# A second matrix product as seven products of combined quarters, in a two-layer graph network kernel

## The chip, the cores and the metric

The kernel runs on one core of one Trainium2 chip. The metric is device microseconds of one execution. The kernel before took 2775.54 us, the median of three runs from 2774.79 to 2775.55. The profile is of one further execution, whose span from the first to the last instruction is 2774.7 us.

## The reference

Two layers are applied to `x`, 16 batches of 1024 nodes with 256 channels, all in fp32. Layer 0 is an attention whose queries come from a weighted adjacency product; it isn't touched. Layer 1 is a graph convolution with two dense products and two batch norms:

```python
agg = jnp.einsum('nm,bmd->bnd', A_hat, features)
x = agg.reshape(-1, d)
h = jax.nn.relu(_batchnorm(x @ W1.T + b1, g1, be1))
out = h @ W2.T + b2
out = _batchnorm(out, g2, be2)
```

`W1` is 512 x 256 and `W2` 256 x 512. The layer's input is added to `out`. The change concerns `h @ W2.T + b2`, which per batch is a product of a 256 x 512 matrix with a 512 x 1024 one, in the transposed form that the kernel uses (channels on the partitions).

## The kernel before, in words

The function `layers` makes layer 0 and the first part of layer 1: adjacency product, `W1` product and bias. It leaves the result in device memory as 32 arrays `y1_d[i]` of 128 x 4 x 512 (two halves of 512 nodes for each of 16 batches, four chunks of 128 hidden channels), and the layer's input as `x1_d[b]`. The statistics for the first batch norm are gathered on the way, on VectorE. The last writes of `y1_d` are issued from the GpSimd queue (line 497).

The function `second` does the rest, and is where the change lies. Its order is the order of the code, as written by hand; each engine works through its own queue in that order and waits on semaphores.

- `affine` (lines 831 to 840) turns mean and variance into scale and shift. Its reciprocal square root runs on GpSimd (lines 80 and 81), three small operations follow on VectorE.
- For each of 32 half batches `i`, `load_y` (line 864, SP queue) brings 1 MB into one of three buffers of pool `io`; `relu` (line 870, ScalarE) applies the batch norm and the ReLU in place, chunk by chunk; `product` (line 878, TensorE) makes two products of 128 output channels x 512 nodes, each a sum over four chunks of `W2`, in one of four PSUM banks. One fp32 matmul of the code appears as two records in the trace. `keep` (lines 889 and 890, VectorE) adds the bias, which moves the result from PSUM to a resident tile `y2`, and takes its statistics.
- On the way five tiles `x1_d[b]` are loaded ahead by `load_x1` (line 850). Those beyond the five use the `io` buffers once these are free.
- Then the second batch norm: `bn_aggr` (line 921), `affine`, and for each batch a scale and shift on ScalarE (line 928), transposes on TensorE (line 940), the sum with `x1` on VectorE (line 946), and one write of 1 MB from the GpSimd queue (line 947). The next `x1` tile is loaded when a write has freed its buffer.

`look` and `flag`, called once in the middle of the loop, test whether layer 0's exponentials stayed in range; a second pass after that test isn't taken in the runs shown.

Of the kernel before, what the change touches and what calls it, by code (L numbers as in the profile page):

```python
# [10 lines left out]
F32 = mybir.dt.float32  # L11
AF = mybir.ActivationFunctionType
ALU = mybir.AluOpType
# [4 lines left out]
P = 128  # L18
# [5 lines left out]
def gnn_two_layers_kernel(  # L24
# [12 lines left out]
    nc = tc.nc  # L37
    B, N, C = x.shape
    H1 = w1_t.shape[1]
    NT = N // P  # L40
    CC = C // P
    HC = H1 // P
    HD = C // HEADS
    FB = 512
    NH = N // FB
# [15 lines left out]
    w2 = const.tile([P, HC, C], F32, name="w2")  # L61
    b1, g1, be1 = (vec[:, i * HC : (i + 1) * HC] for i in range(3))
    b2, g2, be2 = (vec[:, 3 * HC + i * CC : 3 * HC + (i + 1) * CC] for i in range(3))
    stats1 = const.tile([P, HC, B * NH, 6], F32, name="stats1")
    mv1 = const.tile([P, HC, 2], F32, name="mv1")
    stats2 = const.tile([P, CC, B * NH, 6], F32, name="stats2")
# [11 lines left out]
    def rsqrt(dst, src, add, tmp):  # L78

        nc.gpsimd.tensor_scalar_add(tmp, src, add)  # L80
        nc.gpsimd.tensor_tensor(dst, tmp, neg_half[:, : dst.shape[1]], op=ALU.pow)
# [740 lines left out]
    def second(kind):  # L822

        st = ExitStack()
        wp = st.enter_context(tc.tile_pool(name=f"wp_{kind}", bufs=1))
        yp = st.enter_context(tc.tile_pool(name=f"yp_{kind}", bufs=1))
        xp = st.enter_context(tc.tile_pool(name=f"xp_{kind}", bufs=5))
        io = st.enter_context(tc.tile_pool(name=f"io_{kind}", bufs=3))
        ps = st.enter_context(tc.tile_pool(name=f"ps_{kind}", bufs=4, space=PSUM))

        def affine(mv, gamma, beta, name):

            n = mv.shape[1]
            sm = wp.tile([P, 4, n], F32, name=f"sm_{name}")
            s, sh, rstd, tmp = (sm[:, i, :] for i in range(4))
            rsqrt(rstd, mv[:, :, 1], EPS, tmp)
            nc.vector.tensor_mul(s, rstd, gamma)
            nc.vector.tensor_mul(sh, mv[:, :, 0], s)
            nc.vector.tensor_sub(sh, beta, sh)
            return s, sh  # L840

        xos = []

        def load_x1():


            b = len(xos)
            pool, tag = (xp, "xo") if b % 8 < 5 else (io, "yin")
            xo = pool.tile([P, NT, C], F32, tag=tag, name=f"xo_{kind}_{b}")
            nc.sync.dma_start(out=xo, in_=x1_d[b])  # L850
            xos.append(xo)

        with st:
            y2 = [yp.tile([P, CC, N], F32, name=f"y2_{kind}_{b}") for b in range(B)]
            JH = HC // 2
            aff = []
            for half in range(2):
                r = slice(half * JH, (half + 1) * JH)
                aff.append(affine(mv1[:, r], g1[:, r], be1[:, r], f"1{half}"))
            ys, pzs = {}, {}  # L860

            def load_y(i):
                ys[i] = io.tile([P, HC, FB], F32, tag="yin", name=f"yin_{kind}_{i}")
                nc.sync.dma_start(out=ys[i], in_=y1_d[i])

            def relu(i, half):
                s1, sh1 = aff[half]
                for j in range(JH):
                    y = ys[i][:, half * JH + j, :]
                    nc.scalar.activation(  # L870
                        y, y, AF.Relu, bias=sh1[:, j : j + 1], scale=s1[:, j : j + 1]
                    )

            def product(i, k, half):
                if half == 0:
                    pzs[i, k] = ps.tile([P, FB], F32, tag="pz", name=f"pz_{kind}_{i}_{k}")
                for j in range(half * JH, (half + 1) * JH):
                    nc.tensor.matmul(  # L878
                        pzs[i, k],
                        w2[:, j, k * P : (k + 1) * P],  # L880
                        ys[i][:, j, :],
                        start=(j == 0),
                        stop=(j == HC - 1),
                    )

            def keep(i, k):
                b, g = divmod(i, NH)
                dst = y2[b][:, k, g * FB : (g + 1) * FB]
                nc.vector.tensor_scalar_add(dst, pzs[i, k], b2[:, k : k + 1])
                nc.vector.bn_stats(stats2[:, k, i, :], dst)  # L890

            for i in range(3):
                load_y(i)

            for half in range(2):
                for i in range(2):
                    relu(i, half)
                for i in range(2):
                    for k in range(CC):
                        product(i, k, half)  # L900
                        if half == 1:
                            keep(i, k)
            for i in range(2, B * NH):
                if i > 2:
                    load_y(i)
                if i % 4 == 3 and len(xos) < 5:
                    load_x1()
                for half in range(2):
                    relu(i, half)
                for k in range(CC):  # L910
                    for half in range(2):
                        product(i, k, half)
                    keep(i, k)
                if kind == "f" and i == B * NH // 2:
                    look()
                if kind == "f" and i == B * NH // 2 + 3:
                    flag(ps.tile([P, FB], F32, tag="pz", name=f"good_{kind}")[:, 0:1])

            mv2 = wp.tile([P, CC, 2], F32, name="mv2")
            for k in range(CC):  # L920
                nc.vector.bn_aggr(mv2[:, k, :], stats2[:, k].rearrange("p a s -> p (a s)"))
            s2, sh2 = affine(mv2, g2, be2, "2")
            for b in range(B):
                while len(xos) < min(b + 8, B):
                    load_x1()
                xo = xos[b]
                for k in range(CC):
                    nc.scalar.activation(
                        y2[b][:, k, :],
                        y2[b][:, k, :],  # L930
                        AF.Identity,
                        bias=sh2[:, k : k + 1],
                        scale=s2[:, k : k + 1],
                    )
                for g in range(NT // 2):
                    pt = ps.tile([P, 2, C], F32, tag="pz", name=f"pt_{kind}_{b}_{g}")
                    for j in range(2):
                        t = 2 * g + j
                        for k in range(CC):
                            nc.tensor.transpose(  # L940
                                pt[:, j, k * P : (k + 1) * P],
                                y2[b][:, k, t * P : (t + 1) * P],
                                ident,
                            )
                    dst = xo[:, 2 * g : 2 * g + 2, :]
                    nc.vector.tensor_add(dst, pt, dst)
                nc.gpsimd.dma_start(out=out[b].rearrange("(t p) c -> p t c", p=P), in_=xo)  # L947
# [6 lines left out]
    def look():  # L954

        nc.vector.tensor_reduce(ext[:, 0:1], seen[:, 0, :], AX.X, ALU.max)
        nc.vector.tensor_reduce(ext[:, 1:2], seen[:, 1, :], AX.X, ALU.min)
        nc.vector.tensor_scalar(ext[:, 0:1], ext[:, 0:1], 1e25, None, op0=ALU.is_le)
        nc.vector.tensor_scalar(ext[:, 1:2], ext[:, 1:2], 1e-30, None, op0=ALU.is_ge)
        nc.vector.tensor_mul(ext[:, 2:3], ext[:, 0:1], ext[:, 1:2])  # L960

    def flag(good):

        nc.tensor.matmul(good[0:1, :], ext[:, 2:3], ones[:, 0:1], start=True, stop=True)
        nc.vector.tensor_scalar(bad, good[0:1, :], -1.0, float(P), op0=ALU.mult, op1=ALU.add)

    with tc.manual_schedule():
        layers(False)
        second("f")

    again = nc.values_load(bad[0:1, 0:1], min_val=0, max_val=P)  # L971
    with tc.If(again > 0):
        layers(True)
        second("s")
# [37 lines left out]
```

## Time and profile before

| | time, us |
|---|---|
| median of three runs | 2775.54 |
| span of the profiled execution | 2774.7 |
| TensorE busy | 2700.8 (97%) |
| VectorE busy | 1610.3 (58%) |
| ScalarE busy | 1277.1 (46%) |
| GpSimd busy | 190.8 (7%) |
| first matmul of line 878 starts, last one ends | 2467.04, 2689.05 |
| first transpose of line 940 starts | 2695.43 |
| first and last write of line 947 are issued | 2701.05, 2758.33 |

In the profile PE is TensorE's matmul, PEld its weight load, DVE VectorE, ACT ScalarE, POOL GpSimd and SP the queue that issues most loads. A group of instructions is given as line, engine, operation, output <- inputs with partitions x elements and type, a count, and then busy microseconds, mean nanoseconds of one, and the idle time of that engine just before the group, with what ended it. In the timeline each row is a start, a length, engine, line and operation, and in brackets the idle time before it with what ended it. A window gives for each engine the busy microseconds and instructions, then the clock that TensorE was granted, the busy share of the DMA engines and the GB/s moved.

### The profile page before, as it was taken

The page shows a single profiled execution, that of the slowest core. Times are in us where ns is not written, and L with a number is a line of the kernel's source. Part 1 is how long each engine was busy: PE and PEld are TensorE (multiplying, and loading weights), DVE is VectorE, ACT ScalarE, POOL GpSimd, SP SyncE. Part 2 cuts the span into 40 slices and gives each one's busy share as a digit, 9 for nine tenths or more (in the row PEclk, how much of TensorE's full clock was granted, in tenths as well). Part 3 has the DMA queues.
Part 4 walks back from the last instruction along what each step waited for, and adds up shares of the span by engine and source line. Part 5 has one row for each costly group of instructions (what it writes and reads, how often), then busy time and mean ns, then how long its engine had stood idle before and what let it go on. Part 6 is the DMA issues. An engine that isn't in the chain of part 4 may idle for free. (4 is left out here: it accounts for less than half of the span.)

```text
span 2774.7 us, 31770 instructions
## 1 busy us (share of the span) xinstructions
PE 2700.8 (97%) x12426; PEld 999.5 (36%) x12426; DVE 1610.3 (58%) x2426; ACT 1277.1 (46%) x1811; POOL 190.8 (7%) x320
## 2 busy tenths in 40 slices
PE   7999999999999999999999999999999999999984
PEld 3333333333333333333333333333333333334443
DVE  5665655656565656566565656565565656634444
ACT  5654544535353635444453536354443534334443
POOL 0100100000000001000000000010100001100001
PEclk9999999999999999999999999999999999999997
DMA  4612223122232223231322322232313212245449
GB/s 152 208 50 84 99 80 107 73 97 86 92 107 76 95 81 106 84 103 65 105 77 92 106 84 91 85 105 76 107 61 114 77 61 77 96 162 198 167 148 351
DMA packets 106976, 297.35 MB, mean 107 GB/s; under 512 B 9536, under 2 KB 26432, under 8 KB 98624
## 3 DMA queue, kind: packets, MB, share of 16 engines
q1 hardware_dynamic: 88640, 223.91, 23.8%
q0 software_dynamic: 18176, 71.31, 6.8%
q8 instruction: 100, 1.64, 0.2%
q14 instruction: 60, 0.49, 0.1%
HBM read 223.88 MB, written 71.30 MB: 106 GB/s over the span
## 5 line engine op out<-in xcount | busy, mean ns | idle before, releaser
L641 ACT ACTIVATE p<-sc 128x1024 f32<-128x1024 f32 x512 | 496.3, 1021 | 719.4 <-PE sc L633 719.4
L663 DVE TENSOR_TENSOR acc<-acc,p 128x1024 f32<-128x1024 f32 x384 | 469.5, 1223 | 193.0 <-ACT p L641 172.7
L633 PE MATMUL sc<-q,k 64*128 64x512 f32 x2048 | 510.6, 617 | 0.5 <-ACT p L641 0.5
L674 PE MATMUL o<-p,v 128*64 128x512 f32 x2048 | 497.5, 607 | 0.0
L146 PE MATMUL pa<-aht,h_b 128*64 128x512 f32 x2048 | 455.9, 592 | 0.0
L146 PE MATMUL pg<-w,h_a 128*64 128x512 f32 x2048 | 453.5, 592 | 1.1 <-DVE q L401 1.1
L633 PEld LDWEIGHTS sc<-q,k 64*128 64x128 f32 x2048 | 176.6, 186 | 321.8 <-issue 280.8
L146 PEld LDWEIGHTS pg<-w,h_a 128*64 128x64 f32 x2048 | 148.0, 137 | 293.3 <-issue 282.7
L146 PEld LDWEIGHTS pa<-aht,h_b 128*64 128x64 f32 x2048 | 146.9, 137 | 286.6 <-issue 284.3
L700 DVE RECIPROCAL inv<-sums 128x128 f32<-128x128 f32 x256 | 221.7, 917 | 24.5 <-PE sums L691 24.5
L146 PE MATMUL py<-at,w 128*64 128x512 f32 x1024 | 230.6, 592 | 0.8 <-ACT y L496 0.8
L674 PEld LDWEIGHTS o<-p,v 128*64 128x64 f32 x2048 | 124.4, 136 | 286.6 <-issue 286.4
L878 PE MATMUL pz_f<-yin_f,w 128*128 128x512 f32 x512 | 222.0, 596 | 4.1 <-ACT yin_f L870 4.1
L660 DVE TENSOR_TENSOR acc<-p,p 128x1024 f32<-128x1024 f32 x64 | 78.4, 1225 | 247.7 <-ACT p L641 247.7
L354 ACT ACTIVATE w<-cbc,csum 128x512 f32<-128x512 f32 x256 | 170.1, 714 | 75.8 <-PE pg L146 75.7
L496 ACT ACTIVATE y<-py,vec 128x512 f32<-128x512 f32 x128 | 87.6, 684 | 224.9 <-PE py L146 196.5
L366 DVE SCALAR_TENSOR_TENSOR w<-w,adj 128x1024 f32<-128x1024 f32 x128 | 155.2, 1212 | 43.9 <-ACT w L362 43.7
L870 ACT ACTIVATE yin_f<-yin_f,sm 128x512 f32<-128x512 f32 x128 | 93.5, 802 | 119.1 <-DMA yin_f<-y_d 116.6
L878 PEld LDWEIGHTS pz_f<-yin_f,w 128*128 128x128 f32 x512 | 97.7, 191 | 127.6 <-issue 113.0
L362 ACT ACTIVATE w<-w 128x1024 f32<-128x1024 f32 x128 | 134.7, 1052 | 1.7
L146 PEld LDWEIGHTS py<-at,w 128*64 128x64 f32 x1024 | 73.2, 137 | 147.1 <-issue 137.9
L497 POOL DMA_DIRECT2D y_d<-y x128 | 70.7, 553 | 763.6 <-ACT y L496 758.6
(89 smaller groups left out, 1892.5 us busy)
## 6 DMA issues: line engine op xcount, KB each, us to landing
adj<-in_adj_dram SPq DMA_DIRECT2D x128, 512.0 KB, 3.7
aht<-aht_d SPq DMA_DIRECT2D x128, 512.0 KB, 3.6
y_d<-y POOLq DMA_DIRECT2D x128, 256.0 KB, 2.8
yin_f<-y_d SPq DMA_DIRECT2D x32, 1024.0 KB, 4.8
x<-in_x_dram SPq DMA_DIRECT2D x32, 512.0 KB, 4.8
para<-in_para_dram SPq DMA_DIRECT2D x64, 256.0 KB, 3.8
x_d<-x POOLq DMA_DIRECT2D x16, 1024.0 KB, 4.3
xo_f<-x_d SPq DMA_DIRECT2D x16, 1024.0 KB, 7.6
```

The lines of the kernel that those rows point to most:

```text
L146: nc.tensor.matmul(dst[r], left[:, r], right, start=start, stop=stop)
L354: nc.scalar.activation(w[:, t, :], cbc[:, q * FB : (q + 1) * FB], AF.Abs, bias=csum[:, th * TH + t : th * TH + t + 1], scale=-1.0,)
L362: nc.scalar.activation(made[i], made[i], AF.Tanh, scale=-0.5 / C)
L366: nc.vector.scalar_tensor_tensor(w, w, 1.0, a, op0=ALU.add, op1=ALU.mult)
L496: nc.scalar.activation(y, made, AF.Identity, bias=b1[:, j : j + 1])
L633: nc.tensor.matmul(sc[:, e, :], ks[b][k][r, m * P : (m + 1) * P], qs[b][k][r, f * FB : (f + 1) * FB], start=True, stop=True,)
L641: nc.scalar.activation(pr, sc, AF.Exp)
L663: nc.vector.tensor_add(self.acc, self.acc, pr)
L674: nc.tensor.matmul(self.o[r, :], vs[b][k][:, m, r], pr[:, e, :], start=(m == 0), stop=(m == NT - 1),)
L700: nc.vector.reciprocal(self.inv[:, c], self.pt[:, c])
L870: nc.scalar.activation(y, y, AF.Relu, bias=sh1[:, j : j + 1], scale=s1[:, j : j + 1])
L878: nc.tensor.matmul(pzs[i, k], w2[:, j, k * P : (k + 1) * P], ys[i][:, j, :], start=(j == 0), stop=(j == HC - 1),)
```

## The change

The 256 x 512 weight and the 512 x 1024 activations of a batch are each cut into four quarters: `a11, a12, a21, a22` (128 x 256) and `b11, b12, b21, b22` (256 x 512, where the second index is the half batch). With Winograd's form of Strassen's method the four quarters of the result come from seven products, `m1` to `m7`, of quarters and their sums and differences. Each product is a sum over two chunks of 128, so a batch has 14 matmuls of the code where it had 16.

- Weights: `s1` to `s4` are made once, by four GpSimd operations of 128 x 256, ahead of the first `affine` in the code.
- Activations, per batch: `t1 = b12 - b11` (`combine_1`), `t2 = b22 - t1` (`combine_2`), then `t2 = b21 - t2` in place (`combine_4`), on GpSimd; `t3 = b22 - b12` in place of `b12` (`combine_3`) on VectorE. Each is 128 x 1024. For the first batch `combine_1` and `combine_2` are on VectorE.
- Results, per batch: ScalarE moves `m1` out of PSUM with the bias; seven VectorE operations of 512 columns add the other products, where four bias additions stood; the four statistics stay. `b2_step`, the difference of the two bias columns, is made once.
- Order: `graph(b)` makes the products of batch b, and between them advances `ahead_of(b + 1)`, which issues the ReLUs, differences and later loads of the next batches.
- Buffers: `io` has four tiles where it had three, `xp` three where it had five; one more tile `both` of 8 KB a partition serves as t1 and t2 of the last batch and then as an `x1` tile. The other batches' t1 and t2 lie in the place of the last batch's `y2`. PSUM keeps four banks. `x1` loads stand after batches 1, 3 and 5 (one each), 14 and 15 (two each).

The core of the diff:

```diff
-        xp = st.enter_context(tc.tile_pool(name=f"xp_{kind}", bufs=5))
-        io = st.enter_context(tc.tile_pool(name=f"io_{kind}", bufs=3))
+        xp = st.enter_context(tc.tile_pool(name=f"xp_{kind}", bufs=3))
+        io = st.enter_context(tc.tile_pool(name=f"io_{kind}", bufs=4))
...
+            nc.gpsimd.tensor_add(s1, a21, a22)
+            nc.gpsimd.tensor_sub(s2, s1, a11)
+            nc.gpsimd.tensor_sub(s3, a11, a21)
+            nc.gpsimd.tensor_sub(s4, a12, s2)
             aff = []
...
-                for j in range(half * JH, (half + 1) * JH):
+            def combine_1(b, engine):
+                b11, b12, _, _ = inputs(b)
+                second_steps(b)
+                engine.tensor_sub(t1s[b], b12, b11)
+
+            def combine_2(b, engine):
+                engine.tensor_sub(t2s[b], inputs(b)[3], t1s[b])
+
+            def combine_3(b):
+                _, b12, _, b22 = inputs(b)
+                nc.vector.tensor_sub(b12, b22, b12)
+
+            def combine_4(b):
+                nc.gpsimd.tensor_sub(t2s[b], inputs(b)[2], t2s[b])
+
+            def product(name, left, right):
+                made = ps.tile([P, FB], F32, tag="pz", name=f"{name}_{kind}")
+                for j in range(JH):
                     nc.tensor.matmul(
-                        pzs[i, k],
-                        w2[:, j, k * P : (k + 1) * P],
-                        ys[i][:, j, :],
-                        start=(j == 0),
-                        stop=(j == HC - 1),
-                    )
-
-            def keep(i, k):
-                b, g = divmod(i, NH)
-                dst = y2[b][:, k, g * FB : (g + 1) * FB]
-                nc.vector.tensor_scalar_add(dst, pzs[i, k], b2[:, k : k + 1])
-                nc.vector.bn_stats(stats2[:, k, i, :], dst)
+                        made, left[:, j, :], right[:, j, :], start=(j == 0), stop=(j == JH - 1)
+                    )
+                return made
+
+            def graph(b, ahead):
...
+                nc.scalar.activation(
+                    c12, product(f"m1_{b}", a11, b11), AF.Identity, bias=b2[:, 0:1]
+                )
+                m5 = product(f"m5_{b}", s1, t1s[b])
+                next(ahead, None)
+                add(c11, product(f"m2_{b}", a12, b21), c12)
+                stats(0, 0, c11)
+                add(c12, product(f"m6_{b}", s2, t2s[b]), c12)
+                combine_4(b)
+                next(ahead, None)
+                nc.vector.scalar_tensor_tensor(
+                    c21, product(f"m7_{b}", s3, t3), b2_step, c12, op0=ALU.add, op1=ALU.add
+                )
+                add(c12, m5, c12)
+                add(c22, m5, c21)
+                add(c12, product(f"m3_{b}", s4, b22), c12)
+                stats(1, 1, c22)
+                next(ahead, None)
+                add(c21, product(f"m4_{b}", a22, t2s[b]), c21)
+                stats(0, 1, c12)
+                stats(1, 0, c21)
+                next(ahead, None)
+
+            def ahead_of(b):
...
+                for i in range(2):
+                    relu(2 * b + i, 0)
+                yield
+                for i in (1, 0):
+                    relu(2 * b + i, 1)
+                combine_1(b, nc.gpsimd)
+                yield
+                combine_3(b)
+                yield
+                combine_2(b, nc.gpsimd)
+                for i in range(2):
+                    if 2 * b + 2 + i < B * NH:
+                        load_y(2 * b + 2 + i)
+                yield
```

More of the change, by code (lines that the diff above doesn't have):

```diff
@@ L847, in load_x1 @@
             b = len(xos)
-            pool, tag = (xp, "xo") if b % 8 < 5 else (io, "yin")
+            pool, tag = ((xp, "xo"), (io, "yin"), (wp, "both"))[(b % 8 > 2) + (b % 8 > 6)]
             xo = pool.tile([P, NT, C], F32, tag=tag, name=f"xo_{kind}_{b}")
@@ L853, in second @@
         with st:
-            y2 = [yp.tile([P, CC, N], F32, name=f"y2_{kind}_{b}") for b in range(B)]
             JH = HC // 2
+            a11, a12, a21, a22 = (
+                w2[:, k * JH : (k + 1) * JH, c * P : (c + 1) * P] for c in (0, 1) for k in (0, 1)
+            )
+            combined = wp.tile([P, 4, JH, P], F32, name="combined")
+            s1, s2, s3, s4 = (combined[:, i] for i in range(4))
+            nc.gpsimd.tensor_add(s1, a21, a22)
+            nc.gpsimd.tensor_sub(s2, s1, a11)
+            nc.gpsimd.tensor_sub(s3, a11, a21)
+            nc.gpsimd.tensor_sub(s4, a12, s2)
             aff = []
@@ L859, in second @@
                 aff.append(affine(mv1[:, r], g1[:, r], be1[:, r], f"1{half}"))
-            ys, pzs = {}, {}
+            b2_step = wp.tile([P, 1], F32, name="b2_step")
+            nc.vector.tensor_sub(b2_step, b2[:, 1:2], b2[:, 0:1])
+            ys, t1s, t2s, y2 = {}, {}, {}, []
             def load_y(i):
@@ L866, in relu @@
             def relu(i, half):
-                s1, sh1 = aff[half]
+                scale, sh = aff[half]
                 for j in range(JH):
@@ L870, in relu @@
                     nc.scalar.activation(
-                        y, y, AF.Relu, bias=sh1[:, j : j + 1], scale=s1[:, j : j + 1]
+                        y, y, AF.Relu, bias=sh[:, j : j + 1], scale=scale[:, j : j + 1]
                     )
-            def product(i, k, half):
-                if half == 0:
-                    pzs[i, k] = ps.tile([P, FB], F32, tag="pz", name=f"pz_{kind}_{i}_{k}")
-                for j in range(half * JH, (half + 1) * JH):
-                    nc.tensor.matmul(
-                        pzs[i, k],
-                        w2[:, j, k * P : (k + 1) * P],
-                        ys[i][:, j, :],
-                        start=(j == 0),
-                        stop=(j == HC - 1),
-                    )
@@ L886, in keep @@
-            def keep(i, k):
-                b, g = divmod(i, NH)
-                dst = y2[b][:, k, g * FB : (g + 1) * FB]
-                nc.vector.tensor_scalar_add(dst, pzs[i, k], b2[:, k : k + 1])
-                nc.vector.bn_stats(stats2[:, k, i, :], dst)
-            for i in range(3):
-                load_y(i)
[L895 to L914, printed above, removed]
+            def inputs(b):
+                return [ys[2 * b + n][:, k * JH : (k + 1) * JH, :] for k in (0, 1) for n in (0, 1)]
@@ new lines, in second_steps @@
+            def second_steps(b):
+                if b < B - 1:
+                    pair = [
+                        yp.tile([P, JH, FB], F32, tag=f"y2_{B - 1}_{i}", name=f"t{i}_{kind}_{b}")
+                        for i in range(2)
+                    ]
+                else:
+                    both = wp.tile([P, 2, JH, FB], F32, tag="both", name=f"t_{kind}_{b}")
+                    pair = [both[:, i] for i in range(2)]
+                t1s[b], t2s[b] = pair
+            def combine_1(b, engine):
+                b11, b12, _, _ = inputs(b)
+                second_steps(b)
+                engine.tensor_sub(t1s[b], b12, b11)
@@ new lines, in graph, with stats @@
+            def graph(b, ahead):
+                b11, t3, b21, b22 = inputs(b)
+                y2.append(
+                    [
+                        yp.tile([P, N], F32, tag=f"y2_{b}_{k}", name=f"y2_{kind}_{b}_{k}")
+                        for k in range(CC)
+                    ]
+                )
+                c11, c12, c21, c22 = (
+                    y2[b][k][:, g * FB : (g + 1) * FB] for k in range(CC) for g in range(NH)
+                )
+                add = nc.vector.tensor_add
+                def stats(k, g, c):
+                    nc.vector.bn_stats(stats2[:, k, b * NH + g, :], c)
+                nc.scalar.activation(
+                    c12, product(f"m1_{b}", a11, b11), AF.Identity, bias=b2[:, 0:1]
+                )
+                m5 = product(f"m5_{b}", s1, t1s[b])
[7 more added lines that the diff above has]
+                    c21, product(f"m7_{b}", s3, t3), b2_step, c12, op0=ALU.add, op1=ALU.add
+                )
+                add(c12, m5, c12)
[7 more added lines that the diff above has]
+                next(ahead, None)
@@ new lines, in ahead_of @@
+            def ahead_of(b):
+                if b == B:
+                    return
+                for i in range(2):
[12 more added lines that the diff above has]
+                yield
@@ new lines, in second @@
+            for i in range(4):
+                load_y(i)
+            for i in range(2):
+                relu(i, 0)
+            combine_1(0, nc.vector)
+            for i in (1, 0):
+                relu(i, 1)
+            combine_2(0, nc.vector)
+            combine_3(0)
+            for b in range(B):
+                graph(b, ahead_of(b + 1))
+                if b in (1, 3, 5, B - 2, B - 1):
+                    for _ in range(1 + b // (B - 2)):
+                        load_x1()
+                if kind == "f" and b == B // 2:
@@ L915, in second @@
                     look()
-                if kind == "f" and i == B * NH // 2 + 3:
+                if kind == "f" and b == B // 2 + 2:
                     flag(ps.tile([P, FB], F32, tag="pz", name=f"good_{kind}")[:, 0:1])
@@ L928, in second @@
                     nc.scalar.activation(
-                        y2[b][:, k, :],
-                        y2[b][:, k, :],
+                        y2[b][k],
+                        y2[b][k],
                         AF.Identity,
@@ L941, in second @@
                                 pt[:, j, k * P : (k + 1) * P],
-                                y2[b][:, k, t * P : (t + 1) * P],
+                                y2[b][k][:, t * P : (t + 1) * P],
                                 ident,
```

## The prediction

> **What bounds the kernel now.** I read the page's busy shares and 40 slices first (PE busy 97% of the span), then the groups to find the edited stage, then that stage by windows. The page's chain of waits is no help: it ends at the closing branch.
>
> ```profile
> L878 PE MATMUL pz_f<-yin_f,w 128*128 128x512 f32 x512 | 222.0, 596 | 4.1 <-ACT yin_f L870 4.1
> ...
> L870 ACT ACTIVATE yin_f<-yin_f,sm 128x512 f32<-128x512 f32 x128 | 93.5, 802 | 119.1 <-DMA yin_f<-y_d 116.6
> ```
>
> These groups are the stage: 512 matmul records in 222.0 us, with 4.1 us of PE idle, all before the first. ACT idles for its input, but PE never waits for that. The windows:
>
> ```profile
> core 0: us, PE busy (x) PEld busy (x) DVE busy (x) ACT busy (x) POOL busy (x), PEclk, DMA share, GB/s
> 2550.00:2600.00 50.00, 50.00 (x118) 22.18 (x117) 21.32 (x34) 22.28 (x32) 0.00 (x0) 1.00 0.53 189
> ```
>
> PE is busy 50 of 50 us at full clock, DVE and ACT under half, POOL idle, DMA half used. In the output stage the same view shows DMA at share 1.02 (2740 to 2750 us) and PE at 6.47 of 10 us, so there DMA is the bound. A busy PE need not be at its peak, so I take its pitch from its consumer, in the timeline:
>
> ```profile
> 2685.66 0.75 DVE L889 TENSOR_SCALAR y_f<-pz_f,vec 128x512 f32<-128x512 f32 x1 [1.95 <-PE pz_f L878]
> 2686.44 0.69 DVE L890 BATCH_NORM_STATS2 stats<-y_f 128x6 f32<-128x512 f32 x1
> 2689.09 0.75 DVE L889 TENSOR_SCALAR y_f<-pz_f,vec 128x512 f32<-128x512 f32 x1 [1.95 <-PE pz_f L878]
> 2689.88 0.69 DVE L890 BATCH_NORM_STATS2 stats<-y_f 128x6 f32<-128x512 f32 x1
> ```
>
> One product of four weight chunks is evicted every 3.432 us (six starts from 2671.93 to 2689.09), and DVE waits 1.95 us for PE each time. A chunk costs 0.858 us (two records), a batch of 16 chunks 13.73 us, 16 batches 219.6 us; the other 2.4 us of 222.0 are the cold start. **PE bounds this stage.** The head of it:
>
> ```profile
> 2463.95 0.54 POOL L497 DMA_DIRECT2D y_d<-y  x1 [1.08 <-DVE mv L502]
> ...
> 2464.51 0.24 POOL L80 TENSOR_SCALAR sm<-mv 128x2 f32<-128x2 f32 x1
> ...
> 2466.17 4.34 ACT L870 ACTIVATE yin_f<-yin_f,sm 128x512 f32<-128x512 f32 x6 [2.52 <-DVE sm L839]
> ...
> 2467.04 3.71 PE L878 MATMUL pz_f<-yin_f,w 128*128 128x512 f32 x5 [4.12 <-ACT yin_f L870]
> ```
>
> POOL is serial here without a hole: the last write of layer 0 ends at 2464.49, the scale of batch norm 1 starts at 2464.51, and ACT and PE follow it. What is put between these two moves the whole stage.
>
> [...] L663, 1024 elements, takes 1.22 us. On GpSimd this trace has only tiny operations (L81, a power of 128x2, 0.71 us). [...] clock 0.61 from 2467.04 to 2471.40, after the gap of 4.12.
>
> **The change part by part.**
>
> *Removed: two of 16 chunks of each batch.* 16 x 2 x 0.858 = **-27.5 us** of PE, if PE stays the bound at 7 x 1.716 = 12.01 us a batch.
>
> *Added, throughput per batch.* VectorE: six adds of 512 from PSUM (0.69, as L476), one scalar_tensor_tensor (0.69 to 0.75, as L476 and L889; I take 0.75), four bn_stats (0.69), one 1024-wide difference in SBUF (1.22, as L663): 4.14 + 0.75 + 2.78 + 1.22 = 8.9 us. ACT: eight ReLUs at 0.71 to 0.80 (6.4) and the m1 eviction (0.69, as L496): 7.1. GpSimd: three 1024-wide differences; [...] It is unshown here[...]. DMA: 2 MB a batch, 175 GB/s against 408 reached in the output stage. All fit under 12.01, so no engine's sum is the new bound.
>
> *Added waits, with PE at 12.01 a batch.* Products end at 1.7 (m1), 3.4 (m5), 5.1 (m2), 6.9 (m6), 8.6 (m7), 10.3 (m3), 12.0 (m4). I allow 0.2 to 0.3 from a product's end to a consumer's start (L889 shows 0.2).
> - PSUM has four banks for seven products. In the built order m7 waits for the ACT eviction of m1, m3 for the add of m2, m4 for the add of m6: long done. m5 keeps a bank of its own until 11.0, the next m5 wants it at 13.7. No cost.
> - GpSimd: combine_4 (waits for m6) 7.15 to 9.45; m4 wants it at 10.3. combine_1 of the next batch 9.5 to 11.8; its m5 wants it at 13.7. combine_2 waits for m4, whose operand it overwrites: 12.3 to 14.6; the next m6 wants it at 17.15.
> - VectorE: m7's add 8.8, then 9.55, 10.3 (m5 twice), 11.0 (m3), 11.75 (statistics), combine_3 ready at 12.5. [...] Behind it on VectorE stands m4's add, 16.65, and the next m6 wants m4's bank at 17.15. **Slack 0.5 us**: I cost this at nothing, hidden by m1, m5 and m2 of the next batch, but it is the thinnest place.
> - ACT and SP: input tiles come free at 9.45 (combine_4) and 10.5 (m3) and are reloaded. A load of 1 MB lands in 4.8 us median, 11.0 at most, so at 15.3, or 21.5 at worst; with two ReLUs (1.5) and combine_1 (2.4) the operand of the m5 after next is ready by 25.4 at worst, wanted at 25.7. Hidden. The x1 loads stand behind those loads on SP's queue.
>
> *Head.* Four GpSimd operations of 128x256 stand between L497 and L80. [...] **+2.4 us**[...]. They can't start sooner, for they wait behind L497 on POOL, and everything waits behind them. [...] combine_1 of batch 0 on VectorE (1.22 after four ReLUs, 2.9) ends 4.2 after ACT's start, when the cold m1 (4 x 0.86 from 0.87) ends: no gap. The fourth early load, the small b2_step and the earlier x1 issues run under the end of layer 0 or the stage.
>
> *Tail.* Before, the last product's end is followed by 0.75 + 0.69 on VectorE. Now VectorE has the add of m4 and two statistics left, plus about 0.1 of backlog: 0.69 x 3 + 0.1 = 2.2, **+0.75 us**. The output stage keeps its order: eight x1 tiles loaded ahead in both, of which before three and now five arrive around the end of the products, while DMA share is 0.30; I take 0, within 2 us either way. It is DMA-bound, so it moves as a block with its start.
>
> Sum: -27.5 + 2.4 + 0.75 = -24.3 us on the span of 2774.7, 2750.4. The timed runs' median of 2775.54 is 0.8 above that span, so **2751.2**.
>
> **The rivals.**
> *A. The lock and a longer GpSimd difference x eat part of it.* From x = 2.55 on combine_2 starts when POOL is free (7.15 + 2x + 0.1), and if combine_3 loses the race each batch stalls by the excess of 7.25 + 3x + 2.2 over 17.15. x = 2.8 gives 0.7 x 15 = 10.5: **2762**. For it: slack of only 0.5. Against: [...] combine_3 may win the race.
> *B. Slower.* The same chain, m6, three GpSimd differences, the blocked combine_3, m4's add, next m6, becomes the batch's period: 3x + 4.3. It decides against the kernel once the stall passes (27.5 - 3.15)/15 = 1.6 us, that is x above 3.1. At x = 3.2 the stall is 1.9, 28.5 in all: **2780**. For it: GpSimd's price is nowhere in this trace. [...]
> *C. No change: loads are late.* With four tiles for two live batches a load is asked for only when its tile is free. If loads land after 12.7 us, 1.4 us are lost per batch: 2751.2 + 21 = **2772**. Against: 11.0 is the longest seen, and DMA is used less than half.
> *That it doesn't do what it says* is excluded: the built order has 14 chunks a batch where there were 16.
>
> **How the numbers follow.** Forecast 0.75; A 0.13; B 0.07; C 0.05. A measurement of this kernel tells about 0.2% from no change (5.6 us): forecast and A are faster, 0.88; C 0.05; B 0.07. The range goes from 2747 (head at 1.2, tail and output stage kind) to 2763, which takes in A; B and C, 0.12, are left out.
>
> **What would show it.** Right: PE busy 50 of 50 us in the middle, statistics of a batch 12.0 us apart, the first product starting near 2469.5 and the last ending near 2664[...]. Wrong: PE idle before m6 released by VectorE, or before m4 or m5 released by POOL (A, B); idle of ACT for loads that PE shares (C); an output stage that is longer than before's.

## The result and the profile after

The changed kernel took **2747.81 us**, the median of four runs from 2747.41 to 2748.32, against 2775.16 (2774.78 to 2775.55) for the kernel before: 27.35 us less, a ratio of 0.9902 with a 95% interval from 0.9884 to 0.9919. The forecast was 2751.2. The profiled execution has a span of 2746.0 us.

I cut both profiles at the same four marks, all starts or ends of rows in the timeline: the last write of layer 0, the first matmul of the edited stage, the last one, and ScalarE's first operation of the output stage.

| part, us | before | after | difference | forecast |
|---|---|---|---|---|
| last L497 ends, to first matmul (head) | 2.55 | 5.40 | +2.85 | +2.4 |
| first matmul to last (stage) | 222.01 | 194.84 | -27.17 | -27.5 |
| last matmul to ScalarE's scale and shift (tail) | 5.09 | 5.44 | +0.35 | +0.75 |
| from there to the end (output stage) | 80.54 | 77.23 | -3.31 | 0, within 2 |
| all up to the end of L497 | 2464.49 | 2463.08 | -1.41 | untouched |

The last row is scatter: a second profile of the kernel before has 2462.77 there, and later ones of the changed kernel 2463.91 and 2465.10. The other four rows sum to -27.3 us, within 0.1 us of the difference of the timed medians.

The page of the changed kernel, busy time of each engine over the span:

```profile
PE 2672.5 (97%) x12362; PEld 988.0 (36%) x12362; DVE 1651.9 (60%) x2493; ACT 1286.2 (47%) x1827; POOL 312.3 (11%) x370
```

TensorE has lost 28.3 us, VectorE has gained 41.6 and GpSimd 121.5, and the span is 28.7 shorter. What the engines gained lies beside TensorE, as two windows in the middle of the stage show:

```profile
core 0: us, PE busy (x) PEld busy (x) DVE busy (x) ACT busy (x) POOL busy (x), PEclk, DMA share, GB/s
2500.00:2550.00 50.00, 50.00 (x118) 22.09 (x117) 34.57 (x51) 27.83 (x40) 31.06 (x13) 1.00 0.57 221
2550.00:2600.00 50.00, 50.00 (x118) 22.23 (x117) 34.42 (x55) 27.78 (x39) 32.86 (x13) 1.00 0.43 168
```

PE is still busy 50 of 50 us at full clock, with DVE at 34.5 where it had 21.3 and POOL at 32 where it had nothing. One batch in the timeline of the changed kernel (L915 is `combine_4`, L905 `combine_1`, L912 `combine_3`, L908 `combine_2`, L960 the add of m4):

```profile
2549.88 2.37 POOL L915 TENSOR_TENSOR t_f<-yin_f,t_f 128x1024 f32<-128x1024 f32 x1 [3.81 <-PE m_f L920]
...
2552.20 2.36 POOL L905 TENSOR_TENSOR t_f<-yin_f,yin_f 128x1024 f32<-128x1024 f32 x1
...
2552.97 1.88 PE L920 MATMUL m_f<-t_f,w 128*128 128x512 f32 x4
...
2554.65 1.21 DVE L912 TENSOR_TENSOR yin_f<-yin_f 128x1024 f32<-128x1024 f32 x1
2554.69 1.88 PE L920 MATMUL m_f<-yin_f,w 128*128 128x512 f32 x4
...
2555.03 3.04 POOL L908 TENSOR_TENSOR t_f<-yin_f,t_f 128x1024 f32<-128x1024 f32 x1 [0.47 <-PE m_f L920]
...
2555.77 0.68 DVE L960 TENSOR_TENSOR y_f<-m_f,y_f 128x512 f32<-128x512 f32 x1
...
2559.84 1.88 PE L920 MATMUL m_f<-t_f,combined 128*128 128x512 f32 x4
...
2561.89 2.36 POOL L915 TENSOR_TENSOR t_f<-yin_f,t_f 128x1024 f32<-128x1024 f32 x1 [3.82 <-PE m_f L920]
```

L915 comes again after 12.01 us, which is the forecast period. Counted from the batch's start (12.01 before 2554.69, that is 2542.68), `combine_4` runs from 7.2 to 9.6 and m4, its user, starts at 10.3; `combine_2` runs from 12.35 to 15.4 and m6, its user, starts at 17.2. Of the three on GpSimd `combine_4` is the tightest, with 0.72 us to its user. A difference on GpSimd takes 2.36 us, but L908 takes 3.04: VectorE's L912 had started 0.38 us earlier, with both inputs in SBUF. All 15 L908 on GpSimd take 3.045 us or more; L905 and L915, beside which VectorE reads PSUM or runs statistics, stay at 2.35 to 2.42.

The head of the stage in the same kernel's timeline:

```profile
2462.54 0.54 POOL L497 DMA_DIRECT2D y_d<-y  x1 [0.98 <-DVE mv L502]
...
2463.10 0.73 POOL L862 TENSOR_TENSOR combined<-w 128x256 f32<-128x256 f32 x1
2463.91 0.72 POOL L863 TENSOR_TENSOR combined<-combined,w 128x256 f32<-128x256 f32 x1
2464.59 0.72 POOL L864 TENSOR_TENSOR combined<-w 128x256 f32<-128x256 f32 x1
2465.27 0.72 POOL L865 TENSOR_TENSOR combined<-w,combined 128x256 f32<-128x256 f32 x1
2465.96 0.23 POOL L80 TENSOR_SCALAR sm<-mv 128x2 f32<-128x2 f32 x1
...
2468.48 3.78 PE L920 MATMUL m_f<-yin_f,w 128*128 128x512 f32 x4 [7.70 <-ACT yin_f L882]
```

The four weight combinations stand between L497 and L80, as forecast, and fill 2.86 us from 2463.10 to 2465.96.

### The profile page after: what moved, and what is told of

It reads as the page before. It is cut to its first block, busy times and chain, and to the rows that moved or that the text cites. A ratio compares the mean times of both kernels' runs of the same rounds, so it can differ in the third digit from the quotient of the medians.

```text
span 2746.0 us, 31942 instructions
## 1 busy us (share of the span) xinstructions
PE 2672.5 (97%) x12362; PEld 988.0 (36%) x12362; DVE 1651.9 (60%) x2493; ACT 1286.2 (47%) x1827; POOL 312.3 (11%) x370
## 5 line engine op out<-in xcount | busy, mean ns | idle before, releaser
L497 POOL DMA_DIRECT2D y_d<-y x128 | 70.7, 552 | 764.2 <-ACT y L496 759.4
L731 DVE TENSOR_TENSOR x<-ot,x 128x512 f32<-128x512 f32 x64 | 44.3, 692 | 134.9 <-PE ot L727 134.8
L476 DVE TENSOR_TENSOR at<-pa,dbc 128x512 f32<-128x512 f32 x64 | 44.2, 690 | 121.1 <-PE pa L146 121.1
L146 PE MATMUL pv<-kvw,ht 128*64 128x256 f32 x1024 | 116.2, 379 | 0.4 <-DVE v L438 0.4
```

The lines of the kernel that those rows point to most:

```text
L146: nc.tensor.matmul(dst[r], left[:, r], right, start=start, stop=stop)
L497: nc.gpsimd.dma_start(out=y1_d[i][:, j, :], in_=y)
```

## The experiments

### Is the stage's gain the two chunks, and does it repeat?

Both kernels were profiled once more (`before_again`, `after_again`). A third kernel, `chunks16`, is the changed one with the two missing chunks put back: m1 is accumulated over its two chunks twice, so its m1, and with it c11, c12, c21 and c22, are not the layer's values.

```diff
-                for j in range(JH):
+                for j in (0, 1, 0, 1) if name[:2] == "m1" else (0, 1):
```

> The kernel before, profiled a second time. Theory 1 (the output stage is really shorter in the changed kernel): its output stage, from the first scale and shift of line 928 to the end of the span, is again near 80.6 us. Theory 2 (scatter from run to run): it lies anywhere between 77 and 81 us. For layer 0: if the 2 us by which its first line 497 came later than in the changed kernel are scatter, this profile shows another value.

> The changed kernel, profiled a second time. Theory 1: output stage again near 77.2 us. Theory 2: anywhere between 77 and 81 us. Time about 2747.8 us.

> The changed kernel with the two chunks of m1 multiplied twice, so 16 chunks a batch as before and everything else as in the change. If TensorE bounds the stage and nothing else gave the gain: plus 16 x 2 x 0.858 = 27.5 us, 2775.3. Rival (another engine or the loads have become the bound, TensorE has slack): the second pass hides in part, under 2770.

Measured, in a single execution of each: `before_again` 2773.77 (stage 222.01, output stage 79.55), `after_again` 2748.12 (194.92 and 76.55). `chunks16` took 2776.04, ratio 1.0001 [0.9993, 1.001] to the kernel before, and its stage 222.24 us, 27.40 more than the changed kernel's. Its window:

```profile
2500.00:2550.00 50.00, 50.00 (x118) 22.13 (x117) 28.04 (x42) 25.42 (x36) 26.43 (x11) 1.00 0.48 188
```

PE is full again, with all of the combinations still there: 32 chunks cost 27.4 us, and with them back the stage is as long as before to 0.2 us, so the combinations cost it next to nothing. Its time also says more than was asked. Head and tail are 3.2 us longer than before's, so at equal stages it should have been 3 us slower than before; it was equal. Its output stage was 77.09. So the 3 us of the output stage came with the change in the repeated profiles too, and not from the products.

### The weight combinations behind the first batch norm

`weights_late` issues the four combinations after the affine loop, so that L80 follows L497 at once.

```diff
-            nc.gpsimd.tensor_add(s1, a21, a22)
-            nc.gpsimd.tensor_sub(s2, s1, a11)
-            nc.gpsimd.tensor_sub(s3, a11, a21)
-            nc.gpsimd.tensor_sub(s4, a12, s2)
             aff = []
...
+            nc.gpsimd.tensor_add(s1, a21, a22)
+            nc.gpsimd.tensor_sub(s2, s1, a11)
+            nc.gpsimd.tensor_sub(s3, a11, a21)
+            nc.gpsimd.tensor_sub(s4, a12, s2)
```

> The changed kernel with the four weight combinations on GpSimd issued after the two batch norm scales in place of before them. If they stand in the path that opens the stage: minus 4 x 0.69 = 2.8 us, 2745.0, since s1 is then ready about 2.8 us after the scales and m5 wants it 4.3 us after. Rival (something else opens the stage, such as the first loads): no change, 2747.8.

It took 2746.55 us (2745.28 to 2747.24), ratio 0.9893 [0.9877, 0.991]. From the end of L497 to the first ReLU it has 2.07 us where the changed kernel has 4.53, so 2.46 come back; the stage is 0.2 longer. Its timeline:

```profile
2464.28 0.24 POOL L80 TENSOR_SCALAR sm<-mv 128x2 f32<-128x2 f32 x1
...
2466.33 5.76 ACT L882 ACTIVATE yin_f<-yin_f,sm 128x512 f32<-128x512 f32 x8 [2.90 <-DVE sm L839]
...
2469.14 0.73 POOL L869 TENSOR_TENSOR combined<-w,combined 128x256 f32<-128x256 f32 x1
2469.29 1.65 DVE L905 TENSOR_TENSOR t_f<-yin_f,yin_f 128x1024 f32<-128x1024 f32 x1 [0.71 <-ACT yin_f L882]
...
2471.15 1.96 PE L920 MATMUL m_f<-t_f,combined 128*128 128x512 f32 x4 [0.50 <-PE m_f L920]
```

Here GpSimd was first (2469.14) and VectorE's difference took 1.65 us where it takes 1.23. The user of that difference, m5, starts at 2471.15, 0.50 us late. The trace puts this wait down to TensorE itself; that it comes from the difference, which ended at 2470.94, is inferred. L908 of the changed kernel showed the same in the other direction, 3.04 us for 2.36. The head's cost is shown by the marks; of the total time, an interval of 0.17% either way can't tell 2.3 us. The expectation had 2.8.

### How much room has the chain of GpSimd and VectorE?

`combine1_twice` makes `combine_1` twice for every batch but the first, so that one more difference of 2.36 us stands in GpSimd's queue; `all_vector` puts all differences on VectorE.

```diff
                 engine.tensor_sub(t1s[b], b12, b11)
+                if b > 0:
+                    engine.tensor_sub(t1s[b], b12, b11)
```

```diff
-                nc.gpsimd.tensor_sub(t2s[b], inputs(b)[2], t2s[b])
+                nc.vector.tensor_sub(t2s[b], inputs(b)[2], t2s[b])
...
-                combine_1(b, nc.gpsimd)
+                combine_1(b, nc.vector)
...
-                combine_2(b, nc.gpsimd)
+                combine_2(b, nc.vector)
```

> The changed kernel with combine_1 issued twice on GpSimd in each batch but the first, so four differences a batch in place of three. Theory of the chain: combine_4 starts 0.3 after m6, then 3 x 2.33 to the end of the second combine_1, 14.2 against the 13.7 at which the next m5 wants it: a stall of 0.6 to 0.7 us a batch at m5, plus 9 to 10 us, about 2757.5. Rival (only the sum counts, 4 x 2.36 = 9.4 of 12.0 us, so it hides): 2748.

> The changed kernel with all differences on VectorE and none of 1024 columns on GpSimd. VectorE then has its measured 8.3 us a batch plus three differences of 1.2, 11.9 of 12.0 us, in one queue. Theory (the queue order stalls it): combine_2 of the next batch ends near 17.9 where m6 wants it at 17.15, plus 0.7 us or more a batch, 2757 to 2762. Rival (VectorE still fits under TensorE): 2748.

`combine1_twice`: 2759.14 (2758.96 to 2759.26), ratio 0.9943 [0.9925, 0.9961], the stage 206.48 us, 11.6 longer than the changed kernel's or 0.78 for each of 15 batches. GpSimd is not full (40.53 of 50 us in the window from 2500), PE no longer either (48.17). The timeline says which wait it is (L907 is the second `combine_1`, L914 `combine_3`, L910 `combine_2`):

```profile
2544.68 2.36 POOL L905 TENSOR_TENSOR t_f<-yin_f,yin_f 128x1024 f32<-128x1024 f32 x1
...
2547.12 2.34 POOL L907 TENSOR_TENSOR t_f<-yin_f,yin_f 128x1024 f32<-128x1024 f32 x1
...
2549.49 1.23 DVE L914 TENSOR_TENSOR yin_f<-yin_f 128x1024 f32<-128x1024 f32 x1 [2.28 <-POOL t_f L907]
...
2549.51 1.98 PE L922 MATMUL m_f<-t_f,combined 128*128 128x512 f32 x4 [0.46 <-POOL t_f L907]
2549.53 3.40 POOL L910 TENSOR_TENSOR t_f<-yin_f,t_f 128x1024 f32<-128x1024 f32 x1
```

The next m5 waits for the second `combine_1`. In the changed kernel `combine_1` ends 1.85 us before m5 wants it (2554.56 against 2556.41); 2.4 us more overdraw that by some 0.55. From m1 to m5 it is 2.34 us (2547.17 to 2549.51) where a product takes 1.72, and the following m2 comes at 2551.33, 0.1 late once more: 0.72 of the 0.78 us. The period, from one eviction of m1 to the next, is 12.79 us where the changed kernel has 12.02. GpSimd's busy sum, 81%, would have called this free.

`all_vector`: 2753.27 (2752.0 to 2754.84), ratio 0.9923 [0.9905, 0.9941], stage 199.22 us, 4.4 longer than the changed kernel's, and a period of 12.33 us. Its window, and then `combine_2` and the m6 that uses it in its timeline:

```profile
2500.00:2550.00 50.00, 49.73 (x114) 20.95 (x112) 46.85 (x61) 25.89 (x37) 0.00 (x0) 1.00 0.59 222
```

```profile
2548.82 1.21 DVE L908 TENSOR_TENSOR t_f<-yin_f,t_f 128x1024 f32<-128x1024 f32 x1
...
2550.18 1.95 PE L920 MATMUL m_f<-t_f,combined 128*128 128x512 f32 x4
```

VectorE carries all of it at 46.85 of 50 us, but the order of its queue puts `combine_2` behind m4's add and two statistics. It ends at 2550.03, and m6 starts at 2550.18 where 2549.95 was due (m2 started at 2548.23). That is 0.2 us a batch where the expectation had 0.7 or more, because `combine_2` ends only about 0.1 us after m6 was due. So GpSimd's help is worth 4.4 us here, not the whole gain.

### Where do the 3 us of the output stage come from?

The first idea was the arrangement of the `x1` tiles: three instead of five in their own pool, loads after other batches, five loads near the end of the products. `before_x1` gives the kernel before just that.

```diff
-        xp = st.enter_context(tc.tile_pool(name=f"xp_{kind}", bufs=5))
-        io = st.enter_context(tc.tile_pool(name=f"io_{kind}", bufs=3))
+        xp = st.enter_context(tc.tile_pool(name=f"xp_{kind}", bufs=3))
+        io = st.enter_context(tc.tile_pool(name=f"io_{kind}", bufs=4))
...
-            pool, tag = (xp, "xo") if b % 8 < 5 else (io, "yin")
+            pool, tag = ((xp, "xo"), (io, "yin"), (wp, "both"))[(b % 8 > 2) + (b % 8 > 6)]
...
-                if i % 4 == 3 and len(xos) < 5:
+                if i in (3, 7, 11):
...
+                if i in (B * NH - 3, B * NH - 1):
+                    load_x1()
+                    load_x1()
```

> The kernel before, four chunks a product, with the changed kernel's input buffers and x1 loads: three tiles in xp, four in io, one more, loads after half batches 3, 7, 11, and two each after 29 and 31. If the arrangement of the x1 loads is what shortened the output stage by 3.3 us: 2775.2 - 3.3 = 2771.9, output stage near 77.2 us. Rival (it comes from elsewhere, or is scatter): 2775.2.

2777.15 (2775.18 to 2778.45), ratio 1.0006 [0.9997, 1.0015], output stage 79.74. **The idea fell.** (The products' stage was 223.3 us, 1.3 longer; that isn't explained.)

What else differed was where the tiles lie. In the built program the one small tile that the change adds, `b2_step`, takes 32 bytes of a partition and moves all large tiles of `second` by as much, from 224 past a multiple of 256 bytes to a multiple of 256 itself (one of the eight `x1` tiles lies at 192). So a column that nothing reads was added to either kernel:

```diff
+            pad = wp.tile([P, 1], F32, name="pad")
+            nc.vector.memset(pad, 0.0)
```

> The kernel before with one added column tile of 32 bytes a partition ahead of the resident tiles of the last stages, which moves the y2, input and x1 tiles from SBUF addresses that are 32 over a multiple of 64 bytes to multiples of 64, as they lie in the changed kernel. Theory (the address is what shortens the output stage, where the packets of the writes took 46 us of 16 engines' time in the kernel before and 42 in the changed one): output stage about 77.0 in place of 79.9, 2772.5 us. Rival (split y2 tiles or another part of the change does it): 79.9, 2775.4 us.

> The changed kernel with the same 32 bytes added, which moves its y2, input and x1 tiles to 32 over a multiple of 64. Theory of the address: output stage 79.9 in place of 76.9, 2751 us. Rival: unchanged, 2748 us.

`before_shift32` took 2771.31 (21 runs, 2770.53 to 2772.86), ratio 0.9986 [0.9979, 0.9992], its output stage 76.73 us. `after_shift32` took 2753.66 (2751.78 to 2754.4), ratio 0.992 [0.9907, 0.9934], its output stage 80.81. **The same column helps one kernel and harms the other.** The medians moved by 4.2 us down and by 4.8 to 5.9 up (against `after` and `after_third`), the output stages by some 3 to 4 either way; the rest isn't explained. The DMA view from the first output write to the end of the span (queue, packets, MB, share of 16 engines' time), in `before_again`:

```profile
q0 software_dynamic: 4352, 16.78, 63.2%
q1 hardware_dynamic: 1152, 8.39, 28.5%
```

and in `before_shift32`:

```profile
q0 software_dynamic: 4352, 16.78, 60.7%
q1 hardware_dynamic: 1152, 8.39, 30.8%
```

q0 carries the writes out of SBUF, q1 the loads. The writes took 63.2% of 72.71 us, 46.0 us, and then 60.7% of 69.78, 42.4; the loads 20.7 and 21.5. The same packets leave SBUF faster on the whole, and the loads into the same tiles don't gain.

Two kernels then looked for the rule. Both are `weights_late` with a 32-byte column `cpad` among the constants, which moves layer 0's tiles too, and a `pad` in `second`: `late_all_aligned` with one column, `late_all_128` with 24 (96 bytes). A third profile of the changed kernel (`after_third`) stood beside the second.

```diff
+    cpad = const.tile([P, 1], F32, name="cpad")
+    nc.gpsimd.memset(cpad, 0.0)
...
+            pad = wp.tile([P, 24], F32, name="pad")
+            nc.vector.memset(pad, 0.0)
```

> The changed kernel with the weight combinations after the scales, and one 32 byte column added at the outset and one in the last stages, so that layer 0's tiles too lie at multiples of 64 (they lie 32 over in every kernel so far). Layer 0 is bound by TensorE, so the theory expects nothing more there than in the kernel with late weights alone: 2746.5 us. Rival (layer 0's loads and writes stand in its path too): 2 us or more less, below 2744.5 us.

> Late weights, layer 0's tiles moved as in the run before, and 96 bytes in place of 32 in the last stages, so that the x1 tiles lie at multiples of 128 again (there they had come to lie 64 over). If 128 bytes is the step that counts: the first write lands after 4.7 us and the output stage takes 77.0 us again, against 5.15 and 80.4, total 2745.6 us. Rival (64 would have been enough, and the slow output stage had another cause): output stage 80.4, 2749 us.

> The changed kernel once more, timed on the same chip as the kernel with late weights and 128 byte addresses: 2748.0 us; the difference to that one is the worth of issuing the weight combinations late, expected 2.2 us.

`late_all_aligned` took 2748.96 (2747.83 to 2750.63), ratio 0.9902 [0.9887, 0.9918]; `late_all_128` 2749.15 (2747.75 to 2749.79), 0.9905 [0.9888, 0.9921]; `after_third` 2748.88 (2747.72 to 2749.55), 0.9904 [0.9887, 0.992]. So neither multiples of 64 nor of 128 were enough: the head gave its 2.8 us back, and the output stage took it again; `late_all_128` came out 0.3 us slower than `after_third`, where 2.2 faster was expected. Both kernels move layer 0's tiles too, and no run tells that apart at 64 and 128; `after_shift32` has as slow an output stage without it. All profiles together, by the place of the `x1` tiles (in the kernels that descend from the changed one, the tile of batches 7 and 15 lies elsewhere):

| x1 tiles past a multiple of 256 bytes | kernels | output stage, us | time of the writes, us |
|---|---|---|---|
| 0 (one of eight at 192; none in `before_shift32`) | after, after_again, after_third, weights_late, chunks16, combine1_twice, all_vector, before_shift32 | 76.3 to 77.2 | 42.3 to 42.5 |
| 224 | before, before_again, before_x1 | 79.55 to 80.54 | 45.8 to 46.1 |
| 32 (one of eight at 224) | after_shift32 | 80.81 | 45.5 |
| 64 (one of eight at 0) | late_all_aligned | 80.37 | 45.1 |
| 128 (one of eight at 64) | late_all_128 | 80.68 | 45.6 |

The last line, in `late_all_128`, from its first write at 2674.24 to 2748.0:

```profile
q0 software_dynamic: 4352, 16.78, 61.8%
```

**With most tiles on a multiple of 256 bytes the stage was fast, with most at 32, 64, 128 or 224 past one it was slow.** The same view says when the time is lost. Near the end only writes run, and the compute engines are idle (in `before` from 2758.3 to 2766.3 PE, DVE and ACT are busy 0.00 of 8 us, in `after` from 2730 to 2738 too); first `before_again` from 2756 to 2764, then `before_shift32` from 2753.3 to 2761.3:

```profile
q0 software_dynamic: 706, 2.71, 99.6%
q0 software_dynamic: 825, 3.18, 101.5%
```

In 8 us the DMA engines move 2.71 MB out of tiles at 224 and 3.18 MB out of tiles at 0, 17% more. While loads run beside the writes, here from 2725 to 2745 in both, there is no such difference, 2.46 and 2.49 us of all 16 engines for a MB:

```profile
q0 software_dynamic: 924, 3.56, 43.8%
q0 software_dynamic: 1032, 3.98, 49.6%
```

So the place counts where writes run alone (2.71 against 3.18 MB in 8 us), and since nothing computes there, that leaves the source of the writes, the `x1` tiles, and not the `y2` or input tiles that moved with them.

**One tile speaks against a rule of 256.** The last write of the changed kernel, batch 15, reads the tile at 192. In `after_again` that is all that is left from 2738.8 on (280 packets and 1.06 MB to the end, where one write has 272 and 1.05). Its first 2 us:

```profile
q0 software_dynamic: 201, 0.79, 99.2%
```

That is 2.51 us for a MB, as fast as from tiles at 0 (2.55 above) and not as slow as from tiles at 224 (2.94).

From tiles at 0 the runs show 17% more MB in 8 us where writes run alone; over the whole stage the writes from the slow places take 6 to 9% more time (45.1 to 46.1 us against 42.3 to 42.5). The reading by 256 was formed after the last run: no run was made with that forecast. **That the place of the tiles makes the difference is shown; by what rule and why stays open.**

## Why the prediction was right, and where it was not

- **Removed chunks: -27.5, measured -27.17.** The pitch of 0.858 us read from VectorE's evictions held: `chunks16` gives 27.40 for 32 chunks. PE bounded the stage before, and bounds it still.
- **No new bound from the added work: right.** The time of a difference on GpSimd was an assumption of the author that no trace of the kernel before shows; it is 2.36 us, and the recorded times of `combine_4`, `combine_1` and m4 came out within 0.1 us. That the slack was real is shown by `combine1_twice`, where 2.36 us more on GpSimd overdrew it and cost 11.6 us.
- **The thin place of 0.5 us: the race went the other way.** The step supposed that `combine_2` starts first and VectorE's `combine_3` stands, also an assumption that no trace of the kernel before shows. `combine_3` was ready at 12.0, not 12.5, because a run of short VectorE operations goes at a pitch of 0.60 to 0.61 us and not at their durations of 0.69. So it starts 0.4 us ahead, and `combine_2` takes 0.68 us longer. m4's add comes at 13.1 us of the batch, not 16.65, and `combine_2` keeps 1.8 us to m6. Rival A needed both a difference above 2.55 us and a lost race; neither came. Rival B's point, 3.1 us for each difference, was not reached: only L908, with L912 beside it, takes 3.04 (one of 15 takes 3.44). Rival C's loads did make ScalarE idle (12 waits, 13.9 us in all), PE never: its one wait in the stage is the 7.7 us ahead of the first matmul.
- **Head: +2.4, measured +2.85.** The place was right. The term, an assumption too, was small: each of four operations of 128x256 advances the queue by 0.68 to 0.81 us. Moved away (`weights_late`), 2.46 us came back.
- **Tail: +0.75, measured +0.35.** The term was too large, by VectorE's pitch and by a backlog of 0.1 that isn't there. The timeline of the changed kernel has the add of m4 with a wait for PE ahead of it, and then the two statistics:

```profile
2663.36 0.69 DVE L960 TENSOR_TENSOR y_f<-m_f,y_f 128x512 f32<-128x512 f32 x1 [0.16 <-PE m_f L920]
2663.97 1.27 DVE L940 BATCH_NORM_STATS2 stats<-y_f 128x6 f32<-128x512 f32 x2
2665.16 1.88 DVE L1006 BATCH_NORM_AGGREGATE mv<-stats 128x2 f32<-128x192 f32 x2
```

  From the add's start to the aggregate is 1.80 us, where the sum had 2.07 and 0.1. That head and tail together missed by nearly nothing (+0.45 and -0.4) is luck: two misses that cancel.
- **Output stage: 0 within 2, measured -3.3. This is the step that failed.** It counted tiles, loads and their order, and these gain nothing there, as `before_x1` shows. It did not ask where the tiles lie. A 32-byte tile moved most of them to multiples of 256 bytes, and the same move gives the kernel before some 3 us in this stage and 4.2 in all. Head, stage and tail sum to -24.0 us, where the forecast had -24.3; against `before_shift32` (2771.31, not timed side by side) it is about -23.5. That the total came to -27.35 is owed to the addresses.

The fastest kernel measured is `weights_late`, at 2746.55. `late_all_128` lost in the output stage what it had in the head, and moving layer 0's tiles gained nothing that can be told from scatter: the last L497 ends at 2464.2 us there, and at 2465.3 in `late_all_aligned`.

## What to carry to other kernels

A product that PE bounds gains what leaves PE (here 27.17 us of stage for 32 chunks of 0.858), provided that the added chain, not each engine's busy sum, fits in the new period: work it out as deadlines from the product that wants each operand, with the pitch of operations in a row (here 0.60 us on VectorE where the trace gives each 0.69). When a small tile is added, see where the large ones behind it come to lie: here multiples of 256 bytes were good for tiles that DMA writes out of SBUF (output stage 76.3 to 77.2 us), and four of the five other places tried were not (79.55 to 80.81). Compare kernels only at equal places: 32 bytes moved the kernel before by 4.2 us. What one engine does once between two stages cost its whole length here, because the next stage's first step stood behind it in the same queue: 2.86 us on GpSimd made the head 2.85 longer.

## What the runs showed of the hardware

- 1 MB writes out of SBUF took 42.3 to 42.5 us of all DMA engines for 16.78 MB with most tiles at multiples of 256 bytes, and 45.1 to 46.1 with most at 32, 64, 128 or 224 past one. Where writes run alone, 8 us moved 2.71 MB from 224 and 3.18 MB from 0, 17% more; beside loads a MB took 2.46 and 2.49 us. A write from 192 was not slow (2.51 us for a MB). Loads of 8.39 MB were not slower into tiles at 224 (20.7 us) than at 0 (21.5).
- In three cases, where a GpSimd and a VectorE operation that both read two inputs in SBUF overlapped, the one that started later took longer: GpSimd's 2.36 us became 3.04 and, in `combine1_twice`, 3.40; VectorE's 1.23 became 1.65 in `weights_late`. Beside VectorE operations that read PSUM or ran statistics, GpSimd's stayed at 2.35 to 2.42 in the changed kernel. Each time the added 0.68, 1.04 and 0.42 us are some 0.15 less than the time for which the two operations overlap until the first ends (0.83, 1.19, 0.58).
- VectorE operations of 512 columns in a row followed each other at 0.60 us (L955 to L940, from 2552.24 to 2554.05 in `after`), though the trace gives each 0.68 to 0.69.
- A two-input fp32 operation on GpSimd took 2.36 us for 1024 elements and 0.72 for 256: from these two, an estimated 2.1 ns an element and 0.17 us of start.
